# Two-pass attention sums with GRU steps woven into the second pass, in a four-layer graph network kernel

## The chip, the cores and the metric

The kernel runs on one core of one Trainium2 chip. The metric is the device time of one execution in microseconds (us). The four compute engines are PE (TensorE, matrix products), DVE (VectorE), ACT (ScalarE) and POOL (GpSimd); SP issues DMA transfers.

## The reference

`x` holds 3327 nodes with 64 features, `adj` is a dense 0/1 matrix over the nodes. Four layers follow each other, each adding to `x` a function of `h = relu(layernorm(x))`. The change concerns layer 2, a gated graph attention. Since `adj` has no negative entry, its reference comes down to this:

```python
d   = jnp.diag(adj)
A   = adj - jnp.diag(d)
sup = A @ h                                     # sums over neighbours
edge_output = gru_cell(sup, h, w_ih_e, w_hh_e, ...)
edge_support = (sup @ W_gat) / deg              # softmax over equal scores
node_output = gru_cell(edge_support, h, w_ih_n, w_hh_n, ...)
x = x + d[:, None] * (edge_output + node_output)
```

with

```python
r = sigmoid(ir + hr); z = sigmoid(iz + hz); n = tanh(inn + r * hn)
gru_cell = (1 - z) * n + z * h
```

## The kernel before

The nodes are padded to 26 tiles of 128. Rows of `adj` have become masks of one byte per element in SBUF by the time layer 2 runs. Its function is `plain_gat` (L1744), called at the end of layer 1. The two halves of the nodes lie on partitions 0 to 63 and 64 to 127 ("pairs"), so that a tile of 128 partitions by 1664 columns holds all nodes by 64 features; the columns fall into C = 4 column groups of BK = 416.

PSUM is four slots of two banks each (L582). `banks` (L1736) lists the eight banks: 0 and 1 are one slot, 2 and 3 the next, and so on. Column groups 0 to 3 of the sums stand in banks 0 to 3, so groups 0 and 1 share a slot and groups 2 and 3 share the next.

**The sums.** `block(n)` (L1760) adds the contribution of one of the 26 row blocks: two f16 parts of `h`, four column groups, two halves, 16 matmuls of 416 columns (L1766). The blocks run one after the other; `todo` (L1839) hangs other work behind some of them: the correction of the degrees for the diagonal (`degrees`, L1778), the inverse degree (`inverse`, `inverse2`, with a table load on ACT), the weights of the second GRU multiplied by `W_gat` (`weights2`, `weights3`) and the transposed `h` (`turn`, L1813: up to four PE transposes into one bank, then five copies out of it by ACT).

**The GRU.** There are eight steps u, `steps` (L1853): first the four column groups with the edge weights (g = 0), then the four with the node weights (g = 1). Ahead of them `take(k)` copies group k of the sums into the input of the first GRU and `mean(k)` multiplies it by the inverse degree in `deg`; `take2(k)` copies that mean into the input of the second. A step has `products` (L1875: eight f32 products, L1882 into the banks of the two sigmoid gates, L1887 into two more), `sigmoids` (ACT), `before_tanh` (DVE, L1900 and L1901), `tanh` (ACT, L1904) and `state` (DVE, three operations with g = 0, four with g = 1, L1911 to L1915). Step u takes the four banks `(4 + 4 * u + i) % 8`, so two steps share all eight. The loop (from L1936) issues `tanh` and `state` one step later than the products they belong to.

**X.** `last(i)` (L1924) transposes up to four tiles of the result (L1271, in `from_pairs`, L1261), multiplies them by the diagonal (`use`, L1921) and adds them to X (L1922). Parts 0 and 1 (tiles 0 to 7) follow step u = 7 of the loop, parts 2 and 3 (tiles 8 to 12) follow u = 8. When X is complete, layer 3 begins with its mean over X (L434, DVE).

The order on every engine's queue in this stretch is that of the code; a framework adds the semaphore waits, by tiles in SBUF and by slots in PSUM. The code ahead of the loop is

```python
for k in (2, 3):
    mean(k)
for k in (0, 1):
    take(k)
take(3, V)
for k in (0, 1):
    mean(k)
take(2)
```

Of the kernel before, what the change touches and what calls it, by code (L numbers as in the profile page):

```python
# [14 lines left out]
AF = mybir.ActivationFunctionType  # L15
# [6 lines left out]
P = 128  # L22
T = 26
NP = T * P
D = 64
# [23 lines left out]
def tile_gnn4(ctx: ExitStack, tc: tile.TileContext, x, adjT, att0, b0, w1, bias1, w_gat, a_gat,  # L49
# [1337 lines left out]
    def plain_decay(e, right, masks, zo, wt, bias, gru, ball_of_r, then):  # L1387
# [15 lines left out]
        with ExitStack() as st:  # L1403
# [53 lines left out]
            def check(k):  # L1457
                zeros(same, adjs[k], zo[:, k:k + 1])
                release(k)
# [201 lines left out]
            for k in range(LAG, K_ + 1):  # L1661
                c, b = steps[min(k, K_ - 1)]
                if k == T:
                    counts(k - 1, 1, rest)
                    degrees(0, 1)
                    sum_next()
                    for o in range(2):
                        counts(k, o, after)
                        weights(k, o)
                    out_of(0)  # L1670
                elif k == K_:
                    counts(k - 1, 1, rest)
# [12 lines left out]
                if k < K_:  # L1685
                    counts(k, 0, rest)
                    if b == 0:
                        degrees(c, 0)
                if k in (LAG, LAG + 2, LAG + 5):
                    next(norm)  # L1690
                if k in (LAG + 3, LAG + 4):
                    load(next(coming), spares[k - LAG - 3])
                i = k + LEAD
                if EARLY + 8 <= i < K_:
                    (make_mask if i < TAIL[0] else mask_only)(i)
                if EARLY + 8 <= k + 1 < TAIL[0]:
                    check(k + 1)
                if K_ - 3 <= k < K_:
                    check(TAIL[k - K_ + 3])
                t0 = 4 * (k - 18)  # L1700
                if 0 <= t0 < T:
                    with_bias(slice(t0, min(t0 + 4, T)))
                t0 = k - T + 1
                if 0 <= t0 < T and t0 % 2 == 0:
                    n = 2
                    G.tensor_tensor(diag[:, t0 * P:(t0 + n) * P].rearrange("p (t i) -> p t i", i=P),
                                    ident[:, None, :].to_broadcast([P, n, P]),
                                    dcol[:, t0:t0 + n, None].to_broadcast([P, n, P]), op=OP.mult)
                if k == 40:
                    for _, bt, brz in gru:  # L1710
                        G.tensor_tensor(brz, bt[:, :3], bt[:, 3:], op=OP.add)
                    ball_of_r()
                if k in (T + 3, T + 6):
                    t0 = k - T - 3
                    pt = acc[0][:, t0 // 3, :3 * P].rearrange("p (t h d) -> p t h d", h=2, d=D)
                    from_pairs(None, outP, add, wt, range(t0, t0 + 3), pt)
                if k - 2 >= T:
                    b = steps[k - 2][1]
                    drop_diagonal(masks[b // 2][:, b % 2, :], b, 0, NP)
                if k == T - 2:  # L1720
                    A.preload_act_table_set("natural_log_exp_and_others")
                if k > T + 6:
                    next(norm0, None)
# [20 lines left out]
    def plain_gat(masks, zo, deg, first, wg, gru, H, parts, banks, last_x, finish, close):  # L1744
# [5 lines left out]
        HP = NP // 2  # L1750
        C = HP // BK
        C2 = T // 2
        with ExitStack() as st:
            def bank(k):
                return banks[k]
# [1 line left out]
            acc = [bank(k)[:, :BK] for k in range(C)]  # L1757
            order = [o * C2 + k for ks in (range(T // 4), range(T // 4, C2)) for k in ks for o in range(2)]

            def block(n):  # L1760
                b = order[n]
                mask = masks[b // 2][:, b % 2, :]
                for i, w in enumerate([p[:, b % C2, b // C2, :] for p in parts]):
                    for k in range(C):
                        for o in range(2):
                            PE.matmul(acc[k][o * D:(o + 1) * D, :], w,  # L1766
                                      mask[:, o * HP + k * BK:o * HP + (k + 1) * BK],
                                      start=n == 0 and i == 0, stop=n == T - 1 and i == 1)
# [9 lines left out]
            def degrees(k, to):  # L1778
                cs = slice(k * BK, (k + 1) * BK)
                V.tensor_sub(deg[:, cs], deg[:, cs], diagonal(k, to))  # L1780
# [18 lines left out]
            for _ in range(1):  # L1799
                before = st.enter_context(ExitStack())  # L1800
                tp = before.enter_context(room(name="pgn", bufs=1))
                def weights2(to):
                    pt = bank(to)
                    PE.transpose(pt[:D, :D], wg, ident[:D, :D])
                    A.activation(wgT, pt[:D, :D], AF.Copy)
# [4 lines left out]
                    PE.matmul(pt[:D, :3 * D], wgT, wx[:D, :, :].rearrange("k g m -> k (g m)"), start=True, stop=True)  # L1810
                    A.activation(wx[:D, :, :].rearrange("k g m -> k (g m)"), pt[:D, :3 * D], AF.Copy)

                def turn(t0, to):  # L1813

                    n = min(4, C2 - t0)
                    pt = bank(to)
                    for k in range(n):
                        PE.transpose(pt[:, k * P:(k + 1) * P], H[:, t0 + k, :, :].rearrange("p o d -> p (o d)"), ident)
                    cs = slice(t0 * P, (t0 + n) * P)
                    A.activation(hP[:, cs], pt[:, :n * P], AF.Copy)  # L1820
                    for g in range(2):
                        for o in range(2):
                            A.activation(xh[g][o][D:, cs], pt[o * D:(o + 1) * D, :n * P], AF.Copy)

                few, r0 = [tp.tile([P, HP], F32, name=n) for n in ("few", "r0")]

# [8 lines left out]
                def inverse2():  # L1835
                    V.scalar_tensor_tensor(deg, deg, -1.0, r0, op0=OP.mult, op1=OP.mult)
                    V.scalar_tensor_tensor(deg, deg, 2.0, r0, op0=OP.add, op1=OP.mult)

                todo = {3: lambda: degrees(2, 4), 4: lambda: degrees(3, 6), 12: lambda: (weights2(4), inverse()),  # L1839
                        13: lambda: turn(0, 6), 15: lambda: weights3(5), 17: inverse2, 19: lambda: turn(4, 7),  # L1840
                        20: lambda: turn(8, 4), 23: lambda: turn(12, 6)}
                V.tensor_scalar(zo[:, 2 * T:2 * T + 2], zo[:, 2 * T:2 * T + 2], first, None, op0=OP.mult)
                for n in range(3, T):
                    block(n)
                    if n in todo:
                        todo[n]()

# [2 lines left out]

                steps = [(g, k) for g in range(2) for k in range(C)]  # L1853
                K = len(steps)
                pg, gates, nns = {}, {}, {}

                def take(k, on=A):
                    cs = slice(k * BK, (k + 1) * BK)
# [16 lines left out]
                def products(u):  # L1875
                    g, k = steps[u]
                    cs = slice(k * BK, (k + 1) * BK)
                    wx = gru[g][0]
                    pg[u] = pr, pz, ph, pi = [bank((4 + 4 * u + i) % 8)[:, :BK] for i in range(4)]
                    for i, to in enumerate((pr, pz)):  # L1880
                        for o in range(2):
                            PE.matmul(to[o * D:(o + 1) * D, :], wx[:, i, :], xh[g][o][:, cs], start=True, stop=True)  # L1882
                    for o in range(2):

                        for to, q in ((pi, o), (ph, 1 - o)):
                            r = slice(0, D) if to is pi else slice(D, P)
                            PE.matmul(to[q * D:(q + 1) * D, :], wx[r, 2, :], xh[g][q][r, cs], start=True, stop=True)  # L1887
# [31 lines left out]
                def use(t0, n, src):  # L1919
                    o = tp.tile([P, 2, 4, D], F32, name="x", bufs=2)  # L1920
                    V.tensor_mul(o[:, :, :n, :], src, d2[:, :, t0:t0 + n, None].to_broadcast([P, 2, n, D]))  # L1921
                    V.tensor_add(X2[:, :, t0:t0 + n, :], X2[:, :, t0:t0 + n, :], o[:, :, :n, :])  # L1922

                def last(i):  # L1924
                    from_pairs(None, oP, use, None, range(4 * i, min(4 * i + 4, C2)),
                               banks[4 + i].rearrange("p (t h d) -> p t h d", h=2, d=D))

                for k in (2, 3):
                    mean(k)
                for k in (0, 1):  # L1930
                    take(k)
                take(3, V)
                for k in (0, 1):
                    mean(k)
                take(2)
                for u in range(K + 2):  # L1936
                    if u < K:
                        products(u)
                        sigmoids(u)
                    if 0 <= u - 1 < K:  # L1940
                        tanh(u - 1)
                    if u < K:
                        before_tanh(u)
                    if u < C:
                        take2(u)
                    if 0 <= u - 1 < K:
                        state(u - 1)
                    for i in {C + 3: (0, 1), C + 4: (2, 3)}.get(u, ()):
                        last(i)

    def load():
# [101 lines left out]
```

## Time and profile before

| | us |
|---|---|
| median of 3 runs (731.35 to 732.65) | 732.11 |
| the profiled execution's own time | 730.23 |
| its span, first to last instruction | 728.5 |
| first matmul of the sums (L1766) | 381.8 |
| end of the sums | 428.9 |
| first product of the GRU (L1882) | 429.15 |
| end of the last product | 449.3 |
| X complete (end of the last L1922) | 465.65 |
| median duration of L1900 / L1901 / L1904 | 0.65 / 0.59 / 0.64 |
| one multiply or add of a part of X, 512 columns | 0.69 |
| one ACT copy out of PSUM, 64 x 416 (L1862) | 0.51 |

Times inside the span are microseconds from its start. A row of the timeline merges equal instructions that follow each other; what stands in brackets is the engine's idle time just ahead and what ended it. In the chain of work, each piece is what held up the next.

### The profile page before, as it was taken

Reading aid. Unit: us, or ns where it says so; the run is one execution under the profiler, and the core shown is the slowest. Engines: PE = TensorE matmul, PEld = TensorE weight load, DVE = VectorE, ACT = ScalarE, POOL = GpSimd, SP = SyncE. Lnnn points to the kernel's source line nnn. Section 1 sums busy time; section 2 is a strip of 40 time slices with the busy share of each in tenths; the row PEclk is TensorE's granted clock in tenths of the full one; section 3 lists DMA queues with packets and bytes.
Section 4 is the critical chain, followed back from the end, with each engine's and each line's share of the span. In section 5 each row is a group of like instructions: output and inputs, shape, how many; then the busy total and the mean of one; then the engine's idle time right before and its main releaser. Section 6 shows DMA issues by size and latency. Waiting matters only on the chain.

```text
span 728.5 us, 11966 instructions
## 1 busy us (share of the span) xinstructions
PE 632.3 (87%) x4227; PEld 256.4 (35%) x4227; DVE 542.6 (74%) x999; ACT 536.7 (74%) x691; POOL 430.8 (59%) x326
## 2 busy tenths in 40 slices
PE   0899999999999798989998997169999999999940
PEld 0622233333333243434445642042223333333310
DVE  6867778777787799999645339887667877777656
ACT  2688888888888785687871586258888889888831
POOL 2699999989999202116620000048887887888820
PEclk9999999999999999999999999579999999999985
DMA  3988898898888706489940000203334444444001
GB/s 63 334 259 279 263 274 256 279 298 261 267 260 273 274 26 226 132 289 358 403 162 2 1 1 1 94 19 93 94 94 133 115 117 138 120 118 116 2 3 50
DMA packets 61494, 119.25 MB, mean 164 GB/s; under 512 B 9552, under 2 KB 33776, under 8 KB 61424
## 3 DMA queue, kind: packets, MB, share of 16 engines
q1 hardware_dynamic: 57072, 118.38, 51.1%
q10 hardware_dynamic: 4352, 0.02, 0.3%
q8 instruction: 35, 0.57, 0.3%
q14 instruction: 35, 0.29, 0.1%
HBM read 115.64 MB, written 0.88 MB: 160 GB/s over the span
## 4 chain that ended last, share of the span: by engine, by line
PE 64%; DVE 12%; issue 6%; POOL 6%; ACT 5%; DMA 4%; SPq 1%; ACTq 1%; POOLq 0%; DVEq 0%
PE slot L630 16%; PE slot L638 9%; PE slot L611 9%; PE slot L1467 8%; PE slot L612 7%; POOL sig L600 6%; PE slot L1766 5%; PE slot L1481 5%; DMA adj<-in 3%; ACT sig L598 2%; PE slot L1882 1%; DVE X L1520 1%; ACTq L307 1%; DMA own<-in 1%; DVE sig L621 1%
## 5 line engine op out<-in xcount | busy, mean ns | idle before, releaser
L621 DVE SCALAR_TENSOR_TENSOR sig<-slot,sig 128x768 f32<-128x768 f32 (+1 forms) x208 | 212.7, 1023 | 105.7 <-POOL sig L600 105.6
L617 ACT ACTIVATE slot<-slot 128x768 f32<-128x768 f32 (+1 forms) x208 | 177.3, 853 | 53.3 <-PE slot L612 53.0
L600 POOL TENSOR_TENSOR sig<-adj,sig 128x768 f32<-128x768 f32 (+1 forms) x104 | 201.1, 1960 | 14.5 <-ACT sig L598 11.5
L598 ACT ACTIVATE sig<-leftB,right 128x768 f32<-128x768 f32 (+1 forms) x208 | 203.3, 977 | 0.1
L600 POOL TENSOR_TENSOR sig<-mask,sig 128x768 f32<-128x768 fp8e4 (+1 forms) x104 | 173.2, 1678 | 40.5 <-ACT sig L598 35.1
L630 PE MATMUL slot<-sig,Xr 128*64 128x384 f32 (+1 forms) x832 | 169.3, 526 | 5.8 <-DVE sig L621 5.7
L611 PE MATMUL slot<-XC,XT 128*128 128x384 f16 (+1 forms) x416 | 142.2, 342 | 3.1 <-ACT sum L648 1.7
L612 PE MATMUL slot<-XF,XE 73*128 73x384 f16 (+1 forms) x416 | 141.4, 340 | 0.0
L638 PE MATMUL slot<-sig,X 128*32 128x384 f32 (+1 forms) x832 | 94.2, 525 | 0.0
L1473 ACT ACTIVATE w<-slot,ebias 128x832 bf16<-128x832 f32 x76 | 69.0, 952 | 26.3 <-PE slot L1467 25.9
L630 PEld LDWEIGHTS slot<-sig,Xr 128*64 128x64 f32 x832 | 49.8, 135 | 87.1 <-issue 62.0
L611 PEld LDWEIGHTS <-XT 128*128 128x128 f16 x416 | 40.7, 98 | 93.8 <-issue 67.4
L1467 PE MATMUL slot<-mask,rest 128*128 128x416 fp8e4 x208 | 53.9, 341 | 5.7 <-ACT adj L1473 3.5
L1467 PE MATMUL slot<-mask,after 128*128 128x416 fp8e4 x208 | 53.4, 339 | 1.3 <-DVE deg L1491 1.3
L612 PEld LDWEIGHTS <-XE 73*128 73x128 f16 x416 | 40.7, 98 | 29.5 <-issue 5.4
L1362 DVE TENSOR_SCALAR_CACHE_REDUCE same<-late 128x832 fp8e4<-128x832 f32 x48 | 48.4, 1009 | 0.0
L204 POOL TENSOR_TENSOR mask<-mask,offdiag 128x128 fp8e4<-128x128 fp8e4 x26 | 16.5, 645 | 46.1 <-PE slot L1467 46.1
L421 POOL MEMSET X<- 128x832 f32 x2 | 1.6, 792 | 69.4 <-DVE o L1911 69.4
L1766 PE MATMUL slot<-mask,own 128*64 128x416 fp8e4 x416 | 39.8, 346 | 2.2 <-DVE deg L1491 2.2
L638 PEld LDWEIGHTS slot<-sig,X 128*32 128x32 f32 x832 | 16.4, 108 | 67.7 <-issue 66.1
L1481 PE MATMUL slot<-w,h 128*64 128x416 bf16 x304 | 34.0, 345 | 0.0
L527 PE MATMUL pt<-ident_h,Xp 128*64 128x128 f16 x32 | 2.6, 313 | 35.5 <-ACT Xp L466 35.5
(323 smaller groups left out, 681.0 us busy)
## 6 DMA issues: line engine op xcount, KB each, us to landing
adj<-in SPq DMA_DIRECT2D x78, 384.0 KB, 4.8
late<-in SPq DMA_DIRECT2D x48, 416.0 KB, 3.2
adj<-in SPq DMA_DIRECT2D x17, 832.0 KB, 8.4
adj<-in SPq DMA_DIRECT2D x27, 512.0 KB, 5.1
ahead<-in SPq DMA_DIRECT2D x14, 832.0 KB, 6.4
ahead<-in SPq DMA_DIRECT2D x16, 416.0 KB, 5.6
own<-in SPq DMA_DIRECT2D x16, 416.0 KB
own<-in SPq DMA_DIRECT2D x8, 832.0 KB
```

The lines of the kernel that those rows point to most:

```text
L598: A.activation(sig, leftB[c], AF.Sigmoid, bias=right[:, b:b + 1])
L600: G.tensor_tensor(sig, adj, sig, op=OP.mult)
L611: PE.matmul(L[:, o, :c[1] * P], XT[:, rows], XC[c][:, o, :], start=True, stop=False)
L612: PE.matmul(L[:, o, :c[1] * P], XE[:KE, rows], XF[c][:, o, :], start=False, stop=True)
L617: A.activation(L, L, AF.Arctan, scale=PA / SX ** 2)
L621: V.scalar_tensor_tensor(sig, slot[:, :, :tiles[k][0][1] * P], PC, sig, op0=OP.add, op1=OP.mult)
L630: PE.matmul(acc[c][o * D:(o + 1) * D, 0, :n], Xr[:, b, :], sigs[k][:, o, :], start=b == 0, stop=b == T - 1)
L638: PE.matmul(acc[c][q:q + 32, 1, :n], X0[:, b - 1 + i, :], w[:, o, :], start=b == 1, stop=b == T - 1, tile_position=(0, q))
L1467: PE.matmul(cnt[o][:, h, :BK], w, cols(k, o, h), start=w is after and steps[k][1] == T - 1, stop=True, skip_group_check=True)
L1473: A.activation(ws[k][:, o, :, :], cnt[o][:, :, :BK], AF.Exp, scale=-LN2, bias=ebias)
L1481: PE.matmul(acc[c][o * D:(o + 1) * D, h, :BK], parts[i][:, b, :], w[:, o, h, :], start=b == T - 1 and i == 0, stop=b == 0 and i == 1)
L1766: PE.matmul(acc[k][o * D:(o + 1) * D, :], w, mask[:, o * HP + k * BK:o * HP + (k + 1) * BK], start=n == 0 and i == 0, stop=n == T - 1 and ...
```

## The change

The 26 blocks are cut at FULL = 12. Blocks 0 to 11 add to all four column groups as before; blocks 12 to 25 first add to groups 0 and 1 alone. Then `takes` prepares groups 0 and 1, and their four GRU steps begin, with the second halves of the 14 blocks (groups 2 and 3) set ahead of the products of steps u = 0 to 4: 4, 3, 3, 3 and 1 of them. At u = 4 `takes` prepares groups 2 and 3, whose four steps follow. The order of the steps is therefore (g, k) = (0,0), (0,1), (1,0), (1,1), (0,2), (0,3), (1,2), (1,3).

As banks 2 and 3 are still summing, the steps go round three slots, two for each step (RING). X is updated in parts of tiles 0 to 3, 4 and 5, 6 to 8, 9 to 12; the first two follow u = 5, the third u = 7, the fourth u = 8, all in the slot of banks 2 and 3. The work that hangs behind the blocks is placed anew, and one `turn` copies with DVE. In layer 1, the three checks of the last loaded quarters (`check`, DVE) each come one step later.

```diff
-                if K_ - 3 <= k < K_:
-                    check(TAIL[k - K_ + 3])
+                if k > K_ - 3:
+                    check(TAIL[k - K_ + 2])
...
-            def block(n):
+            def block(n, ks=range(C)):
...
-                    for k in range(C):
+                    for k in ks:
...
-                todo = {3: lambda: degrees(2, 4), 4: lambda: degrees(3, 6), 12: lambda: (weights2(4), inverse()),
-                        13: lambda: turn(0, 6), 15: lambda: weights3(5), 17: inverse2, 19: lambda: turn(4, 7),
-                        20: lambda: turn(8, 4), 23: lambda: turn(12, 6)}
+                todo = {3: lambda: (degrees(2, 4), weights2(6)), 10: lambda: (degrees(3, 5), inverse()),
+                        12: lambda: turn(0, 6), 16: lambda: (inverse2(), turn(4, 4, V)),
+                        22: lambda: weights3(7), 23: lambda: turn(8, 6), 25: lambda: turn(12, 5)}
                 for n in range(3, T):
-                    block(n)
+                    block(n, range(C) if n < FULL else range(C // 2))
...
-                steps = [(g, k) for g in range(2) for k in range(C)]
+                halves = range(C // 2), range(C // 2, C)
+                steps = [(g, k) for ks in halves for g in range(2) for k in ks]
...
+                RING = 2, 3, 0
...
-                    pg[u] = pr, pz, ph, pi = [bank((4 + 4 * u + i) % 8)[:, :BK] for i in range(4)]
+                    pg[u] = pr, pz, ph, pi = [bank(2 * RING[(2 * u + i // 2) % 3] + i % 2)[:, :BK] for i in range(4)]
...
+                groups = range(0, 4), range(4, 6), range(6, 9), range(9, C2)
+
                 def last(i):
-                    from_pairs(None, oP, use, None, range(4 * i, min(4 * i + 4, C2)),
-                               banks[4 + i].rearrange("p (t h d) -> p t h d", h=2, d=D))
+                    from_pairs(None, oP, use, None, groups[i],
+                               banks[2 + i % 2].rearrange("p (t h d) -> p t h d", h=2, d=D))
...
+                def takes(ks):
+                    take(ks[0])
+                    for k in ks:
+                        mean(k)
+                    take(ks[1])
+
+                blocks = iter(range(FULL, T))
+                between = {0: 4, 1: 3, 2: 3, 3: 3, 4: 1}
+                takes(halves[0])
                 for u in range(K + 2):
+                    for _ in range(between.get(u, 0)):
+                        block(next(blocks), halves[1])
+                    if u == 4:
+                        takes(halves[1])
                     if u < K:
                         products(u)
                         sigmoids(u)
...
-                    for i in {C + 3: (0, 1), C + 4: (2, 3)}.get(u, ()):
+                    for i in {5: (0, 1), 7: (2,), 8: (3,)}.get(u, ()):
                         last(i)
```

More of the change, by code (lines that the diff above doesn't have):

```diff
@@ L1752, in plain_gat @@
         C2 = T // 2
+        FULL = 2 * (T // 4)
         with ExitStack() as st:
@@ L1811, in weights3, with turn @@
                     A.activation(wx[:D, :, :].rearrange("k g m -> k (g m)"), pt[:D, :3 * D], AF.Copy)
-                def turn(t0, to):
+                def turn(t0, to, on=A):
                     n = min(4, C2 - t0)
@@ L1819, in turn @@
                     cs = slice(t0 * P, (t0 + n) * P)
[L1820 to L1823, printed above, removed]
+                    copies = [(hP[:, cs], pt[:, :n * P])]
+                    copies += [(xh[g][o][D:, cs], pt[o * D:(o + 1) * D, :n * P]) for g in range(2) for o in range(2)]
+                    for to, src in copies:
+                        if on is V:
+                            V.tensor_copy(to, src)
+                        else:
+                            A.activation(to, src, AF.Copy)
                 few, r0 = [tp.tile([P, HP], F32, name=n) for n in ("few", "r0")]
@@ L1922, in use @@
                     V.tensor_add(X2[:, :, t0:t0 + n, :], X2[:, :, t0:t0 + n, :], o[:, :, :n, :])
+                groups = range(0, 4), range(4, 6), range(6, 9), range(9, C2)
                 def last(i):
-                    from_pairs(None, oP, use, None, range(4 * i, min(4 * i + 4, C2)),
-                               banks[4 + i].rearrange("p (t h d) -> p t h d", h=2, d=D))
[L1928 to L1935, printed above, removed]
+                    from_pairs(None, oP, use, None, groups[i],
[8 more added lines that the diff above has]
+                takes(halves[0])
                 for u in range(K + 2):
+                    for _ in range(between.get(u, 0)):
+                        block(next(blocks), halves[1])
+                    if u == 4:
+                        takes(halves[1])
                     if u < K:
@@ L1943, in plain_gat @@
                         before_tanh(u)
-                    if u < C:
-                        take2(u)
+                    if u < K and steps[u][0] == 0:
+                        take2(steps[u][1])
                     if 0 <= u - 1 < K:
                         state(u - 1)
-                    for i in {C + 3: (0, 1), C + 4: (2, 3)}.get(u, ()):
+                    for i in {5: (0, 1), 7: (2,), 8: (3,)}.get(u, ()):
                         last(i)
```

## The prediction

> **What bounds the kernel now.** I read the page's head first, then the chain of work that ended last over the changed stage (381 to 466 us), then the timeline of that stage, then the clock by stretches.
>
> ```profile
> span 728.5 us, 11966 instructions
> PE 632.3 (87%) x4227; PEld 256.4 (35%) x4227; DVE 542.6 (74%) x999; ACT 536.7 (74%) x691; POOL 430.8 (59%) x326
> ```
>
> PE leads over the whole span, but the stage decides. The chain there (start us, us, what):
>
> ```profile
> 425.96 2.95 PE slot L1766 x32
> 428.94 1.09 DVE deg L1868 x2
> ...
> 444.49 1.57 PE slot L1882 x8
> 446.15 0.62 ACT gate L1894
> 446.82 0.65 DVE nn L1900
> ...
> 457.23 0.61 DVE x L1921
> 457.88 1.13 PE slot L1271 x4
> 459.04 0.70 DVE x L1921
> ```
>
> PE is the bound to 428.94 (sums, L1766), then the GRU steps: PE's 2.41 us each (1.55 at L1882, 0.86 at L1887) until 446, then DVE: its steps u=4 to 7 start (L1900) at 443.88, 446.82, 450.26 and 453.70, so 2.94 us with g=0 (five operations) and 3.44 with g=1 (six). X is ready at 465.65. The timeline shows two waits that the change will meet again:
>
> ```profile
> 431.21 1.05 ACT L1862 ACTIVATE xh<-slot 64x416 f32<-64x416 f32 x2 [0.52 <-DVE xh L1864]
> 457.88 1.33 PE L1271 MATMUL slot<-ident,own 128*128 128x128 f32 x5 [3.57 <-DVE x L1921]
> 384.58 2.27 PE L1766 MATMUL slot<-mask,own 128*64 128x416 fp8e4 x12 [2.24 <-DVE deg L1491]
> ```
>
> In the first, ACT's read of one bank waits for DVE's read of the other bank of the same two-bank slot. In the second, PE's transposes for one part of X wait until DVE has read the part before, again in the other bank of one slot. In the third, 12 matmuls take 2.27 us, not 12 x 0.088 = 1.05. The clock by stretches (the third column from the right is PEclk) says why the last happens, and when it happens again:
>
> ```profile
> 386.00:389.00 3.00, 3.00 (x20) 2.06 (x18) 0.35 (x1) 0.00 (x0) 0.00 (x0) 0.66 0.00 0
> 429.00:449.40 20.40, 19.93 (x128) 5.94 (x128) 18.30 (x33) 18.12 (x35) 1.36 (x5) 1.00 0.00 1
> 449.40:465.70 16.30, 3.70 (x13) 2.10 (x13) 14.34 (x27) 1.89 (x3) 0.00 (x0) 0.61 0.22 75
> ```
>
> After 2.2 us without matmuls the clock was at half until about 388.3; after the last products (449.3) it fell at about 453.
>
> **What the Trainium skill says.** "TensorE: Matmul & The Clock Gate", Part 1, gives one idle window of some 3.4 us as what halves PE's clock, and a busy one of that length as what restores it. The trace agrees (3.6 us from 449.3 to the fall), and shows that a window with about 1.1 us of work in it (382 to 385) is idle enough. "PSUM — Partial Sum Buffer", under "PSUM bank collisions raise a hardware error", holds that two engines must not touch one bank and quadrant at once, reads included; the trace agrees in that such reads are put one after the other, and is stricter: the two banks of a slot are. The same page, "Engine vs sequencer instructions", has ACT, DVE and POOL as strict queues and matmuls in program order, so what stands behind a waiting instruction waits too; the 0.52 us above passed on to the gates at 432.29.
>
> **The change part by part.**
>
> *Two passes.* The last 14 blocks do column groups 0 and 1, then 2 and 3. A block is 16 matmuls of 0.0878 us, 1.405; a half is 0.70. No matmul is added. First pass: 428.94 - 14 x 0.70 = 419.1 us if PE never waits. Each turn from fp8 blocks to f32 products costs about 0.13 (48 matmuls took 4.34, not 4.21); four more of them: 0.5.
>
> *The moved preparation.* The third degree correction goes behind block 10, so ACT's chain begins at 406.6: 1.66 + 1.60 + 1.60, table load and probe 1.5, copies of the first transpose 3.0: 416.0. The product of the weights (weights3) now goes into bank 7, the slot whose bank 6 ACT still copies from; PE comes to it at 415.2 and waits 0.9. One group of five copies goes to DVE: 0.60 to 0.69 each by the rows for 512 columns, 3.1 us, ending near 418.5, in DVE's gap (12.7 us idle before L1868) and 1 us before PE wants that slot for the last transposes. I cost it at nothing; were it slower by over 1 us, PE would wait for the rest. ACT's last copies (3.0 + 1.4) end at 422.6, the first take at 423.7. PE, done with four half blocks at 422.4, starts the first products at 423.3: a wait of 0.9.
>
> *Weaving.* A step's period is 2.41 + 3 x 0.70 + 0.13 = 4.65 on PE, against at most 3.44 on DVE and 2.7 on ACT: PE-bound, and the DVE work of four steps is hidden. Products of u=3 start at 423.3 + 3 x 4.65 = 437.3, and the second pass ends at 440.4.
>
> *The hand-over at u=4.* takes() orders four operations on one slot: take(2) on ACT, both means on DVE, take(3) on ACT. The gates of u=4 stand behind take(3) on ACT, and the means behind state(2) on DVE, which ends at 443.4. So: take(2) 440.7 to 441.7, products 441.4 (PE waits 1.0), means 443.3 to 444.4, take(3) to 445.45, gates, and the fifth L1900 at **446.1**, against 443.88 before. Products of u=5 wait for take(3) too. From here both kernels have the same DVE work left: four half-steps before tanh, states 3 to 7 with 18 operations, and X. So the stage is 2.2 us behind here; the PE stalls have eaten the hidden work, because PE has the same sums and products to do in either order, and what DVE needs beyond PE is only 0.5 to 1 us a step.
>
> *X in four parts.* Parts 0 and 1 move from u=7 to u=5, both in one slot. Part 1's transposes wait until DVE has multiplied part 0 (end 453.2), and the products of u=6 now stand behind them on PE; before, all products had been issued. DVE is through with part 1 at 455.0. PE starts these products at 454.0: at full clock L1900 of u=6 comes at 456.5, a wait of 1.5. PE however has had only four transposes since 447.6, some 6 us, so I take half clock for part of it, as at 384.9: one window of 3.4 us, which costs 1.6 more. L1900 of u=6 at **458.1**, DVE idle 3.1. The bounds of the cold part are 0 and 2.4 (all products at half).
>
> *End.* u=7 2.94 later, 461.0; state(6) to 464.5; part 2 waits for its transposes (1.4) and takes 1.1; state(7) 2.35; part 3 transposes 1.7, then 1.4: X at 472.3. The same arithmetic gives 466.4 for the kernel before, where 465.65 was measured (cold transposes counted too dearly in both), so the difference is what I use: **+5.9**, namely 2.2 at the hand-over, 3.1 before u=6 and 0.6 in waits for the transposes of parts 2 and 3. Elements multiplied per part sum to the same.
>
> *The later tail check.* One check (1.87 us) goes behind the second degree copy on DVE. DVE idled 7.1 us before the first copy and 4.1 after, and one check stays between the two copies, so PE's 2.24 us wait stays: nothing. If it moved, 1.9 either way. No DMA is added; the loads of the next stage (SP, issued at 460.98 when their buffers come free) go later by a few us, needed only past 480. After X the program is as before, and PE is cold there in both.
>
> Sum against the profiled execution: span 728.5 + 5.9 = 734.4, time 730.23 + 5.9 = 736.1; it lies 1.9 under the median of 732.11, so the median goes to 738.0.
>
> **Rivals.** *Warm products:* the transposes keep the clock up, or a window falls well. For it: the 384.9 fall came after 2.2 us with nothing at all. Against: one transpose in 3.4 us is less work than the 1.1 us found insufficient. +5.9 - 1.6 - 0.3 = +4.0: 736.1. *Colder still:* waits at u=4 (1.0 and 1.1 us) share a window and products 4 and 5 slow too, or all of u=6: +8: 740.1. *Faster:* the weaving pays because the hand-over doesn't wait. Place: the gates of u=4 behind take(3). If ACT's and PE's waits from weights3 to take(3) cost nothing, the second pass ends at 428.94 + 4 x 2.54 = 439.1, L1900 of u=4 comes 2.5 later at 441.6, 2.3 before its time now, and with u=6 in time X is 2.3 earlier: 729.8. It decides at L1900 of u=4 before 443.9 together with no DVE wait before u=6. For it: slots might be tracked by bank, so that reads of banks 2 and 3 overlap. Against: both waits shown above. *No change:* the hand-over goes as in this rival (-2.3), but u=6 still waits 1.5 and the transposes 0.6: 731.9.
>
> **How the numbers follow.** Forecast (738.0) 0.55; warm 0.23; colder 0.07; no change 0.05; faster 0.10. A measurement tells about 0.2% (1.5 us) from no change. Slower by more: 0.85; within: 0.05; faster: 0.10. The range leaves out the faster cases and the worst of the colder: 734.3 (warm, with one of PE's two early waits of 0.9 gone and take(3) 0.9 sooner) to 740.3 (all products of u=6 cold, +0.8, and clock windows falling badly, +1.5).
>
> **What would show it.** In the profile after: DVE's L1900 of u=4 idle some 1.9 us, put down to ACT gates, and starting later relative to the end of the sums than here; ACT's take(3) waiting 2 to 3 us for DVE's means; PE's products of u=6 behind transposes that waited 3 us for DVE's x; the L1900 of u=6 idle 1.5 to 3.9 us; PEclk of 0.5 near 452 to 455; X at 470 to 473. Wrong if take(3) runs beside the means, if u=6's products don't wait, or if X is ready before 465.

## The result, and the profile after

| | median us (runs) | ratio to the kernel before, 95% interval |
|---|---|---|
| kernel before | 731.08 (727.1 to 732.65, 10 runs) | |
| changed kernel | 739.13 (733.94 to 740.42, 10 runs) | 1.0106 (1.0082 to 1.013) |

The ratios in this text are not quotients of the medians beside them and can differ from these by about 0.1%.

The changed kernel is slower by about 1%. Its profiled execution took 738.03 us, the span is 736.2 us.

Line numbers shift: in the changed kernel the sums are L1767, a take L1868, a mean L1874, `take2` L1879, the products L1888 and L1893, the sigmoids **L1900**, what comes before tanh **L1906** and L1907, tanh L1910, a state L1917 to L1921, X L1927 and L1928. So L1900 of before is L1906 here. The head of the page says that no engine has noticeably more work (PE had 632.3 us, DVE 542.6):

```profile
span 736.2 us, 11968 instructions
PE 635.4 (86%) x4227; PEld 256.2 (35%) x4227; DVE 545.3 (74%) x1002; ACT 534.3 (73%) x688; POOL 432.8 (59%) x326
```

The loss is therefore in waits. Two places of the timeline hold it. First the hand-over at u = 4 (start, duration, engine, line, what; the bracket is the idle time ahead and what ended it):

```profile
441.23 1.05 ACT L1868 ACTIVATE xh<-slot 64x416 f32<-64x416 f32 x2
441.79 2.15 PE L1888 MATMUL slot<-xh,gw 128*64 128x416 f32 x8 [0.60 <-ACT xh L1868]
443.44 0.59 DVE L1921 TENSOR_TENSOR own<-o,nn 128x416 f32<-128x416 f32 x1
443.95 1.08 DVE L1874 SCALAR_TENSOR_TENSOR deg<-slot,deg 128x416 f32<-128x416 f32 x2
445.06 1.05 ACT L1868 ACTIVATE xh<-slot 64x416 f32<-64x416 f32 x2 [2.78 <-DVE deg L1874]
446.13 1.10 ACT L1900 ACTIVATE gate<-slot,gs 128x416 f32<-128x416 f32 x2
446.77 0.65 DVE L1906 SCALAR_TENSOR_TENSOR nn<-slot,gb,gate 128x416 f32<-128x416 f32 x1 [1.75 <-ACT gate L1900]
```

ACT has copied group 2 by 442.3 and could copy group 3, but that copy stands behind DVE's means, and these behind state(2), which ends at 444.0. ACT waits 2.78 us, its gates for u = 4 stand behind, and DVE then waits 1.75 us for the gates. Each of the two engines waits once for the other. In the kernel before, the fifth step of DVE followed the state ahead of it without a wait:

```profile
443.88 0.65 DVE L1900 SCALAR_TENSOR_TENSOR nn<-slot,gb,gate 128x416 f32<-128x416 f32 x1
```

Second, the parts of X behind u = 5:

```profile
453.89 0.44 PE L1271 MATMUL slot<-ident,own 128*128 128x128 f32 x2 [3.21 <-DVE x L1927]
454.26 3.04 PE L1888 MATMUL slot<-xh,gw 128*64 128x416 f32 x8
454.93 0.42 DVE L1928 TENSOR_TENSOR X<-X,x 128x256 f32<-128x256 f32 x1
457.41 1.10 ACT L1900 ACTIVATE gate<-slot,gs 128x416 f32<-128x416 f32 x2 [5.97 <-PE slot L1888]
458.50 0.65 DVE L1906 SCALAR_TENSOR_TENSOR nn<-slot,gb,gate 128x416 f32<-128x416 f32 x1 [3.15 <-PE slot L1893]
```

The two transposes of part 1 wait 3.21 us for DVE's read of part 0, the products of u = 6 stand behind them on PE, and these eight take 3.04 us and not 1.56 or 1.62. Before, all products stood ahead of the first transposes, and DVE didn't wait for them:

```profile
444.42 1.62 PE L1882 MATMUL slot<-xh,gw 128*64 128x416 f32 x8
446.83 1.62 PE L1882 MATMUL slot<-xh,gw 128*64 128x416 f32 x8
450.26 0.65 DVE L1900 SCALAR_TENSOR_TENSOR nn<-slot,gb,gate 128x416 f32<-128x416 f32 x1
450.49 0.52 PE L1271 MATMUL slot<-ident,own 128*128 128x128 f32 x3 [1.18 <-ACT gate L1894]
```

The clock by stretches (PEclk is the third column from the right) in the changed kernel says why:

```profile
441.79:454.26 12.47, 7.19 (x38) 2.65 (x39) 10.41 (x19) 6.74 (x13) 1.34 (x5) 1.00 0.00 1
454.26:457.80 3.54, 3.54 (x13) 1.07 (x16) 1.06 (x3) 0.39 (x1) 0.00 (x0) 0.52 0.00 0
```

The clock halves just as the products begin. This agrees with what "TensorE: Matmul & The Clock Gate", Part 1, says of an idle window of some 3.4 us: PE had two short groups of transposes (0.33 and 0.44 us) since 449.1.

**Where the 7.7 us between the two spans lie.** The start of the sums is 1.14 us later (382.95 against 381.8), X is complete 89.04 us after that and not 83.85 (+5.19), and from there to the end it takes 264.21 us and not 262.85 (+1.36). Only the middle term is the changed code's; of the other two the experiments speak.

### The profile page after: what moved, and what is told of

Read it like the earlier page. It is cut to its first block, busy times and chain, and to the rows that moved or that the text cites. A ratio compares the mean times of both kernels' runs of the same rounds, so it can differ in the third digit from the quotient of the medians.

```text
span 736.2 us, 11968 instructions
## 1 busy us (share of the span) xinstructions
PE 635.4 (86%) x4227; PEld 256.2 (35%) x4227; DVE 545.3 (74%) x1002; ACT 534.3 (73%) x688; POOL 432.8 (59%) x326
## 4 chain that ended last, share of the span: by engine, by line
PE 66%; DVE 13%; ACT 8%; issue 4%; POOL 3%; DMA 3%; ACTq 1%; SPq 0%; POOLq 0%; DVEq 0%
PE slot L630 17%; PE slot L638 10%; PE slot L611 9%; PE slot L1467 8%; PE slot L612 8%; PE slot L1481 5%; PE slot L1767 3%; POOL sig L600 3%; DMA adj<-in 3%; ACT sig L598 2%; PE slot L1888 2%; PE pt L502 1%; ACT slot L617 1%; DVE X L1520 1%; ACTq L307 1%
## 5 line engine op out<-in xcount | busy, mean ns | idle before, releaser
L1767 PE MATMUL slot<-mask,own 128*64 128x416 fp8e4 x416 | 40.2, 345 | 2.2 <-DVE deg L1491 2.2
L527 PE MATMUL pt<-ident_h,Xp 128*64 128x128 f16 x32 | 2.6, 313 | 36.6 <-ACT Xp L466 36.6
```

What stands on the lines that cost most here:

```text
L1767: PE.matmul(acc[k][o * D:(o + 1) * D, :], w, mask[:, o * HP + k * BK:o * HP + (k + 1) * BK], start=n == 0 and i == 0, stop=n == T - 1 and ...
```

## A measure for the experiments

The stage as first measured, from the first matmul of the sums to X, turned out to hold a piece of chance. After the 2.24 us in which PE waits for DVE at the start of the sums, the next 12 matmuls take 1.25 us in one profile and up to 2.29 in another, with the same instructions ahead of them; the same kernel gave 2.08 and 1.25, and stages of 89.04 and 87.44. The clock's drop falls on these matmuls, or on what follows them, or (in three profiles) nothing there is slower; the last section shows what decides it. So the table counts **from the start of the third row block** (the first sums that stand behind the second degree correction), where PE is at full clock in every profile. On this measure the changed kernel gives 79.61 and 79.63 and the kernel before, alone and with the moved checks, 74.41 and 74.39. Differences of 0.1 us can be read from it. (Where an expectation below counts from the second row block, its figures are 2.57 higher; where it names a stage of 83 to 92, it counts from the first matmul.)

| us | stage | fifth L1906 | X after the fifth | after X | median, before on the same chip | ratio (95% interval) |
|---|---|---|---|---|---|---|
| before | 74.41 | 52.64 | 21.77 | 262.85 | | |
| changed | 79.61 | 54.39 | 25.22 | 264.21 | 739.13, 731.08 | 1.0106 (1.0082 to 1.013) |
| changed_again | 79.63 | 54.41 | 25.22 | 263.24 | 737.72, 731.64 | 1.007 (1.0049 to 1.0091) |
| checks_only | 74.39 | 52.63 | 21.76 | 262.68 | 731.86, 731.14 | 1.0003 (0.9982 to 1.0025) |
| takes_together | 77.71 | 52.58 | 25.13 | 263.88 | 736.59, 731.14 | 1.0067 (1.0046 to 1.0087) |
| x_parts_late | 76.08 | 54.41 | 21.67 | 264.33 | 734.24, 731.14 | 1.0044 (1.0026 to 1.0061) |
| pe_kept_warm | 78.00 | 54.39 | 23.61 | 262.99 | 734.29, 731.14 | 1.0045 (1.0033 to 1.0057) |
| both_places | 74.26 | 52.59 | 21.67 | 263.00 | 731.72, 731.64 | 1.0004 (0.9984 to 1.0023) |
| slots_and_early_weights | 72.90 | 52.00 | 20.90 | 264.03 | 732.47, 731.64 | 0.9997 (0.9975 to 1.0019) |
| not_woven | 81.09 | 55.21 | 25.88 | 262.94 | 737.98, 731.64 | 1.0075 (1.0046 to 1.0103) |
| before_with_tail | 72.97 | 52.63 | 20.34 | 263.81 | 730.46, 730.87 | 0.9996 (0.9982 to 1.001) |
| before_tail_again | 72.97 | 52.64 | 20.33 | 264.15 | 730.62, 731.09 | 0.9999 (0.9983 to 1.0015) |
| tail_and_early_chain | 78.47 | 58.64 | 19.83 | 262.89 | 736.50, 730.87 | 1.0065 (1.0043 to 1.0087) |
| tail_chain_mended | 70.77 | 50.93 | 19.84 | 263.07 | 728.22, 731.09 | 0.9956 (0.9939 to 0.9972) |

## The experiments

**The hand-over alone.** In the changed kernel both takes are issued ahead of the means:

```diff
 take(ks[0])
+take(ks[1])
 for k in ks:
     mean(k)
-take(ks[1])
```

> The changed kernel with both takes ahead of both means in takes(), so that ACT reads the slot twice in a row and DVE after that. Theory A (the gates of u = 4 stand behind take(3), which stands behind the means): ACT's wait of 2.8 us ahead of the second take goes, L1906 of u = 4 comes some 1.8 us sooner, the first products of the stage 0 to 0.7 sooner, the later wait ahead of u = 6 stays near 3; stage 86.4, some 2.6 shorter, time 736.5. Theory B: the means now late for the second GRU put the wait there, and the stage stays above 88.

The fifth L1906 comes 1.8 us earlier, at 52.58, and X 1.9 earlier. (`takes` is called at both hand-overs; the first gave 0.17 of it, as the first L1906 comes 34.68 us after the third row block and not 34.85.) ACT copies both groups in one stretch while DVE is still at state(2); the means then find the slot free, and DVE's wait at the fifth L1906 is gone:

```profile
440.97 2.13 ACT L1868 ACTIVATE xh<-slot 64x416 f32<-64x416 f32 x4
443.69 1.08 DVE L1874 SCALAR_TENSOR_TENSOR deg<-slot,deg 128x416 f32<-128x416 f32 x2
443.79 1.11 ACT L1900 ACTIVATE gate<-slot,gs 128x416 f32<-128x416 f32 x2 [0.68 <-PE slot L1888]
444.69 0.65 DVE L1906 SCALAR_TENSOR_TENSOR nn<-slot,gb,gate 128x416 f32<-128x416 f32 x1
```

The 2.78 us of ACT went away with the order of four calls, not with another buffer. "PSUM — Partial Sum Buffer", under "PSUM bank collisions raise a hardware error", keeps two engines from one bank and quadrant at a time, and that alone would order these reads: the copy of group 3 stood behind `mean(3)`, which reads the same bank. So this wait doesn't tell whether the order is by slot or by bank. The 3.21 us ahead of the transposes of part 1 do: these write bank 3 while DVE reads bank 2, the other bank of the slot, and they were held all the same. There the kernel's semaphores, which go by slot, are stricter than the page.

**The place of X's first parts alone.**

```diff
-for i in {5: (0, 1), 7: (2,), 8: (3,)}.get(u, ()):
+for i in {7: (0, 1, 2), 8: (3,)}.get(u, ()):
```

> The changed kernel with the first two parts of X put back to u = 7 (parts 0, 1 and 2 there, 3 at u = 8). Stage means first matmul of the sums to X complete: 83.85 us before, 89.05 after the change. Theory A (the placing of the parts makes the products of u = 6 wait): the wait ahead of L1906 of u = 6 goes from 3.15 us to nothing and that instruction comes 2.9 us after the one of u = 5; PEclk stays at 1.0 until the products are done; stage 85.2, some 3.9 shorter, time 735. Theory B (the loss lies in the split itself: more changes between f8 and f32 work, PE waits up to the hand-over): the wait turns up at another place and the stage stays above 88, time above 738.

The fifth L1906 stays at 54.41, X comes 3.5 us earlier, and the way from the fifth L1906 to X (21.67) is that of the kernel before (21.77). Products of u = 6 and 7 are issued before any transpose, as before, and the clock holds until they are done (it falls at 455.5):

```profile
446.79 1.88 PE L1888 MATMUL slot<-xh,gw 128*64 128x416 f32 x8
449.86 1.62 PE L1888 MATMUL slot<-xh,gw 128*64 128x416 f32 x8 [0.33 <-DVE nn L1907]
452.27 0.65 PE L1271 MATMUL slot<-ident,own 128*128 128x128 f32 x4
```

**Warm products.** Parts 0 and 1 stay behind u = 5, but PE gets 14 more products between their transposes, into a bank that nobody reads; they are added work with no use but to keep PE busy.

```diff
-for i in {5: (0, 1), 7: (2,), 8: (3,)}.get(u, ()):
-    last(i)
+for i in {5: (0, 9, 1), 7: (2,), 8: (3,)}.get(u, ()):
+    last(i) if i < 9 else [PE.matmul(bank(4)[:, :BK], ones_bf, masks[0][:, 0, :BK], start=True, stop=True) for _ in range(14)]
```

> The changed kernel with 14 products of 416 columns added on PE, whose result nobody reads, between the transposes of part 0 and of part 1 of X, where PE has nothing to do for some 3 us. Theory A with a half clock (part of the wait ahead of u = 6 is PE at half clock): PEclk stays 1.0 there, the products of u = 6 take 2.4 us instead of 4.1, L1906 of u = 6 comes 1.5 to 1.8 us sooner although PE has more to do; stage 87.0 to 87.4, time 737. If the clock plays no part: stage the same or up to 0.5 longer.

```profile
450.45 2.62 PE L1962 MATMUL slot<-mask,ones_bf 128*128 128x416 fp8e4 x14
453.82 0.44 PE L1271 MATMUL slot<-ident,own 128*128 128x128 f32 x2 [0.75 <-DVE x L1927]
454.19 1.62 PE L1888 MATMUL slot<-xh,gw 128*64 128x416 f32 x8
456.81 0.65 DVE L1906 SCALAR_TENSOR_TENSOR nn<-slot,gb,gate 128x416 f32<-128x416 f32 x1 [1.52 <-PE slot L1893]
```

The products start where they did and take 1.62 us instead of 3.04; DVE waits 1.52 instead of 3.15, and X is 1.6 earlier. So of the 3.45 us that the parts of X cost, 1.6 are the clock and the rest is the place on PE's queue.

**The moved checks alone**, in the kernel before:

```diff
-                if K_ - 3 <= k < K_:
-                    check(TAIL[k - K_ + 3])
+                if k > K_ - 3:
+                    check(TAIL[k - K_ + 2])
```

> The kernel before with only the moved checks of the change (three checks each one step later). Theory A (nothing: DVE had idle time at both places): stage within 0.3 of 83.85, PE's wait of 2.24 us unchanged, time within 0.2% of the kernel before. Rival C (the 1.15 us by which the sums start later in the changed kernel belong to the moved checks): first matmul of the sums about 1 us later, time about 1 us longer.

Stage 74.39, ratio 1.0003: nothing that can be told from noise. Its sums start at 384.05 us, 2.2 later than in the profile of before, and the time is the same within that; the start of the sums moved between 381.28 and 384.85 over all profiles, in no relation to the edits. The +1.14 of the profiled pair is not of the change.

**The changed kernel again.**

> The changed kernel itself once more, beside the kernel before on the same chip, as the measure for the three others. Its stage (first matmul of the sums to X complete) was 89.0 us against 83.9. Theory A (the whole loss that belongs to the change lies in the stage, and what went longer outside it, +1.35 after X and +1.1 ahead of the sums in the profiled pair, is chance of the clock's windows): 736 to 737 beside a 731 of the kernel before, ratio 1.007, stage 89.0. Theory B (some of the 8 us belongs to the change although it lies outside the stage): 739 again, ratio 1.010 or more.

The stage is the same to 0.02 us, and what follows X takes 263.24 us where the first profile had 264.21. So this last figure differs by 1 us between two executions of one kernel. The ratio is the 1.007 of theory A, and the 5.2 us that the stage lost are 0.7% of 731 (the medians differ by 6.1); what the first ratio (1.0106) has beyond it did not come again with the same code. The intervals overlap between 1.0082 and 1.0091.

**Both places at once** (the two diffs above together).

> Both edits at once: take, take, mean, mean at the hand-over, and parts 0 to 2 of X behind u = 7. Theory A (the hand-over and the place of X's parts are the whole loss and add up): the fifth L1906 comes 17.9 us after the first as with the takes together, that of u = 6 without a wait, stage 83.7, about the 83.9 of before; ratio 1.000, 731. Theory B (splitting the sums into two passes costs by itself: the turns between formats on PE and the waits for slots that remain): stage 85 or more, ratio 1.002 or more. Rival that the two losses overlap, so that undoing both gains no more than undoing one: stage 85.4, ratio 1.004.

The stage is 74.26: the two gains (1.9 and 3.5) add up to 5.4, and the kernel is back at the time of before, ratio 1.0004. So the two places are the whole loss, taken net. At the same time splitting and weaving, as they are placed, gain next to nothing: the fifth L1906 is at 52.59 against 52.64, X at 74.26 against 74.41.

**Without weaving.** All 14 half blocks of the second pass ahead of the first products:

```diff
-between = {0: 4, 1: 3, 2: 3, 3: 3, 4: 1}
+between = {0: 14}
```

> The changed kernel with all 14 half blocks of the second pass ahead of the first products (none between the steps); hand-over and parts of X as changed. Theory A (the weaving hides some 2 to 3 us of DVE work under PE, and the wait at the hand-over eats it): without weaving the hidden work comes back, and the wait at the hand-over stays: stage 91 to 92, ratio 1.010. Theory B (what is hidden is lost again entirely at the hand-over, where DVE is let go idle, so weaving or not comes to the same): stage 89 to 90, the same time as the changed kernel within 1 us.

The stage is 1.5 us longer: less than theory A's 2 to 3 and more than theory B's 1; the medians (737.98, and 737.72 for the changed kernel) can't be told apart. The fifth L1906 is only 0.8 later; the other 0.7 comes after it, with products of u = 5 and u = 6 at half clock. So weaving is worth 0.8 us here at the fifth step. Woven or not, DVE is let go idle at the hand-over (1.75 us in both); that most of what the weaving hides was lost there is argued from this, not measured.

**Two waits for slots less.** Both places, the third weights product at block 8, and X's parts in alternating slots:

```diff
-10: lambda: (degrees(3, 5), inverse()),
+8: lambda: weights3(7), 10: lambda: (degrees(3, 5), inverse()),
...
-22: lambda: weights3(7), 23: lambda: turn(8, 6), 25: lambda: turn(12, 5)}
+23: lambda: turn(8, 6), 25: lambda: turn(12, 5)}
...
-banks[2 + i % 2]
+banks[(2, 6, 3, 7)[i]]
```

> Both edits, and two waits for slots taken away besides: the third weights product is moved up to block 8, so that PE no longer meets ACT's copies in its slot, and the parts of X take their banks from two slots in turn (2, 6, 3, 7), so that the transposes of one part do not wait for DVE's reads of the part before. Theory A (every wait on a shared slot was worth its length at the end): stage 1.5 to 1.9 us shorter than with both places alone, some 82, ratio 0.997, 729. Theory B (PE works the same sums and products in either order and the DVE work that the weaving hides is no more than the chain at the end gets back): no shorter than with both places alone, ratio 1.000.

The stage is 1.36 us shorter than with both places alone: 0.6 ahead of the fifth L1906, 0.8 in the waits for transposes. PE then waited for DVE's copies (0.57 us ahead of the last transpose of h) in place of the weights. The whole time doesn't show the 1.5 us by which the stage now lies under that of before: 0.9997, with an interval that reaches to 0.9975.

**The end of the stage, and an earlier chain.** Two edits on top. DVE's work on part 2 of X is put behind the last state, beside the transposes of part 3; and the third degree correction with the inverse goes from block 10 to block 8, with the transposes of h two or three blocks earlier:

```diff
-8: lambda: weights3(7), 10: lambda: (degrees(3, 5), inverse()),
-12: lambda: turn(0, 6), 16: lambda: (inverse2(), turn(4, 4, V)),
-23: lambda: turn(8, 6), 25: lambda: turn(12, 5)}
+8: lambda: (degrees(3, 5), inverse(), weights3(7)),
+10: lambda: turn(0, 6), 14: lambda: (inverse2(), turn(4, 4, V)),
+20: lambda: turn(8, 6), 23: lambda: turn(12, 5)}
...
-for i in {7: (0, 1, 2), 8: (3,)}.get(u, ()):
-    last(i)
+if u == 7:
+    last(0)
+    last(1)
+    last(2, lambda *a: late.append(a))
+if u == 8:
+    last(3, lambda *a: late.append(a))
+    for a in late:
+        use(*a)
```

> The version with other slots and early weights, with two edits more: DVE's multiplication and addition of part 2 of X come after the last state instead of ahead of it, so that they lie beside the transposes of part 3 (DVE waited 1.21 us for these), and the third degree correction with the inverse comes two blocks earlier, so that the copies of the transposed h are done before PE wants their slot (PE waited 0.57). Counted from the second row block of the sums to X complete (after 82.2, before 77.0, other slots 75.5): 75.5 - 1.1 - 0.5 = 73.9, so 3.1 under the kernel before: ratio 0.996, 728.5. Theory A (each wait of the end of the stage is worth its length in the time of the whole): ratio 0.996, interval under 1. Theory B (what the stage gains is lost after it, in the preparation of layer 3): the stage 3 us shorter, X to the end of the span 266 and not 263 to 264, ratio 1.000.

This version lost by a detail. In block 8 the weights product came third, so ACT's copy of it stood behind the inverse's work on ACT, and the transposes of h, in the same slot, waited for that copy; the clock fell during the wait (at 410.9) and came back at 417.7:

```profile
411.82 0.31 ACT L1812 ACTIVATE gw<-slot 64x192 f32<-64x192 f32 x1
412.18 1.12 PE L1819 MATMUL slot<-ident,own 128*128 128x128 f32 x4 [4.98 <-ACT gw L1812]
413.23 5.91 PE L1767 MATMUL slot<-mask,own 128*64 128x416 fp8e4 x40
```

A copy of 0.31 us cost a wait of 4.98 and then 2.2 us more, as 40 matmuls took 5.91 us where the mended kernel needs 3.71. The tail did what it should: 10.51 us from the last L1906 to X against 11.58.

The mended order needs one call moved:

```diff
-8: lambda: (degrees(3, 5), inverse(), weights3(7)),
+8: lambda: (weights3(7), degrees(3, 5), inverse()),
```

> The same as the tail with the early chain, but in block 8 the third weights product comes ahead of the degree correction and the inverse, so that ACT's copy of it (0.3 us) doesn't stand behind ACT's 6.3 us of the inverse and PE's transposes don't wait 5 us for its slot. From the second row block to X complete: other slots 75.5, less 1.07 for the tail (10.51 us from the last L1906 to X, against 11.58) and 0.6 for the earlier chain: 73.8, against 75.5 of the one-pass kernel with this tail and 77.0 of before. Theory A (stage gains are gains of the whole): ratio 0.996 to the kernel before. Theory B (splitting and weaving give nothing): the stage 75.5 and the ratio 1.000.

```profile
403.65 0.32 ACT L1812 ACTIVATE gw<-slot 64x192 f32<-64x192 f32 x1 [2.20 <-PE slot L1811]
439.14 0.65 DVE L1906 SCALAR_TENSOR_TENSOR nn<-slot,gb,gate 128x416 f32<-128x416 f32 x1 [1.46 <-PE slot L1893]
460.86 1.11 PE L1271 MATMUL slot<-ident,own 128*128 128x128 f32 x4 [2.87 <-DVE own L1921]
462.01 0.69 DVE L1927 TENSOR_TENSOR x<-slot,dcol 128x512 f32<-128x512 f32 x1 [0.15 <-PE slot L1271]
```

ACT copies the weights at 403.65, PE has no wait from there to the first products, and DVE's last wait for transposes is 0.15 us and not 1.21. The stage is 70.77, 3.6 us under before; 728.22 us, ratio 0.9956 (0.9939 to 0.9972). This version beats both kernels.

**The same end in the kernel before**, to see what splitting and weaving are worth by themselves: one pass, the four parts of X and their DVE order as in the last diff, in banks 4, 6, 5 and 7.

> The kernel before, one pass and nothing woven, with the same end alone: parts of X as tiles 0 to 3, 4 and 5, 6 to 8, 9 to 12 in alternating slots, DVE's work on part 2 after the last state. DVE waited 0.48 and 0.99 us for transposes there; both go: 77.0 - 1.4 = 75.6 from the second row block to X complete; ratio 0.998, 730. Theory A (two passes with weaving are worth something once the waits are out): the tail with two passes stays 1.5 us or more under this one. Theory B (splitting and weaving are worth nothing by themselves, the tail alone makes the gain): both within 0.5 us of each other in the stage.

> The kernel before with the tail alone once more, beside the mended one on the same chip. Its stage was 1.4 us shorter than before's, its time 0.4 (ratio 0.9996, 0.9982 to 1.001). If a shorter stage is a shorter kernel, 0.998 now, and the mended one 1.7 us under it; if not, 1.000 for both.

The stage is 72.97 in both profiles, 1.44 under before as expected; the times (0.9996 and 0.9999) can't be told from no change, and the 0.998 that was expected lies just outside both intervals, so most of what this stage gained doesn't show in the kernel's time. Against this kernel the mended one has a stage 2.2 us shorter (1.7 of it ahead of the fifth L1906), and its median is 2.4 lower on the same chip (728.22, 730.62). So **two passes with weaving, with the preparation placed for them, are worth some 2 us once nothing waits at the hand-over, at X and in the preparation**.

## Why the prediction was right, and where its sizes were off

It forecast 738.0 us, by two places: the hand-over and the parts of X. Both are shown, by undoing each alone and both together. By its own steps (the third row block starts 1.14 us later in the profile after, which is allowed for):

- *Two passes, moved preparation.* PE waited 0.51 us for the slot of the third weights product and 0.31 at the first products, forecast 0.9 and 0.9. DVE's five copies cost nothing, as forecast.
- *Weaving.* A period is 4.49 us (2.23 for three half blocks, 1.40 and 0.86 for the products, by the chain of work), forecast 4.65. The 0.13 us that each turn from fp8 to f32 was to cost doesn't show here: 2.41 and 24 x 0.0878 already make 4.52. The period is bound by PE as forecast: DVE waits 1.45 us for the products at u = 2 and u = 3.
- *The hand-over.* Forecast +2.2, measured +1.75 (fifth L1906 at 446.77, against 443.88 + 1.14). The chain of causes is the forecast one, operation by operation. Mis-sized by 0.45: the early waits and the period were priced too high. The words "the same DVE work left" from here are off by one operation: in the traces the kernel before still has 19 operations of `state` from its fifth L1900 on and the changed one 18, as state(3) belongs to the second GRU there. These 0.6 us in favour of the change lie behind the fifth L1906.
- *X in four parts.* Forecast 3.1 us of idle DVE before u = 6, measured 3.15; 1.6 for one window at half clock, and taking that away brought 1.63. The waits for the last two parts are 0.99 and 1.21, together 0.73 over the 0.48 and 0.99 of before, forecast 0.6. From the fifth L1906 to X the forecast was +3.7, measured +3.45.
- *The sum.* +5.9 forecast for the stage, +5.2 measured. The measured terms are 1.75, 3.15 and 0.73, less 0.6 for the operation that is no longer left: 5.0.
- *After X, and ahead of the sums.* Here the prediction had nothing, and the profiled pair shows +1.36 and +1.14. That its 738.0 lies only 1.1 under the measured 739.13 is in part luck. The medians differ by 8.05 us, and 5.9 were forecast: the base (732.11, three runs) was 1.03 over the 731.08 of ten runs, the stage was forecast 0.7 too long, and the surroundings came out longer in those runs. In the second measurement (737.72, beside 731.64) the medians differ by 6.1.
- *The checks.* Forecast nothing; measured 1.0003 (0.9982 to 1.0025), no effect that shows.

Of the rivals, "warm products" fell with the clock of 0.52 from 454.26, and its price (1.6) was right; "colder still" fell with the clock of 1.00 from 441.79 to 454.26, "no change" with DVE's 1.75 us at the hand-over. The "faster" rival named its condition: no cost of the waits from the weights to take(3), and u = 6 in time, then X 2.3 us earlier. What it gave as a reason, slots tracked by bank, would not have met it, since mean(3) and take(3) read one bank. With the waits at take(3) and ahead of u = 6 out, but PE's 0.51 us for the weights still there, both_places didn't reach it (-0.15); with the remaining ones out too, the mended kernel is 2.2 us under the one-pass kernel with the same tail. So the mechanism exists, at about the price worked out, and the changed kernel met none of its conditions.

**What stays open.** What follows X takes 262.7 to 263.2 us in eight profiles and 263.8 to 264.3 in six, with nothing between. The clock tells the two groups apart. The preparation of layer 3 starts with PE at half clock, and full clock comes back 3.8 to 5.3 us after its first transposes (L527) in the eight and 8.7 to 9.3 us after them in the six. In the changed kernel's two profiles, for example, eight products (L555) took 2.02 us in one and 1.16 in the other. The same kernel showed both values, but the one-pass kernel with the tail showed the high one twice, and the medians of the kernels with the high value lie on average 1.8 us above what their stages give, those with the low one 0.5 (median, less that of before on the same chip, less the difference of the stages). That looks as if a kernel's own timing made one value likelier. No run here tests that, and it may be where the 1.4 us that the tail gained in the one-pass kernel went.

## What to carry to other kernels

Before work of two engines is woven, write down the order on each queue around the seam: a read that stands behind another engine's read of the same slot hands that engine's delay on to all that is queued behind it (2.78 us here), and a change of call order alone was worth 1.9 us here. A few small matmuls that must wait belong behind the large ones on PE's queue, since ahead of them they cost their wait and then the clock (3.5 us here for six transposes). And a stage should be measured from a point where the clock is known to be full: that brought two profiles of one kernel from 1.6 us apart to 0.02.

## What was not expected of the hardware

- The same 12 matmuls after the same 2.24 us pause took between 1.25 and 2.29 us over the profiles; in two of them the following block paid instead (2.08 and 2.22 us instead of 1.57). The clock records of each profile change on a grid of 3.41 us, and the grid stands differently against the program each time: the changed kernel's two profiles have drops at 385.99 and 453.25 us, 19.7 periods apart. Of the windows of this grid at full clock between 375 and 470 us, over all profiles, the 31 that half clock followed held at most 1.51 us of matmuls, and the other 287 at least 1.66. In the three profiles where nothing was slower, the pause was so divided between two windows that each held 1.80 us or more.
- Keeping PE busy with 2.62 us of products that nobody reads brought 1.63 us in the stage: the only kernel here that became faster by added work.
- How long PE is busy in the trace doesn't settle when the clock comes back. In the preparation of layer 3 the changed kernel's PE was busy for 3.39 of 3.42 us in the window from 488.39 (transposes of 16-bit numbers and products of 6 columns), and the clock stayed at half for another window; in its second profile 3.38 us of the same kind of work from 487.38 were enough.
